# Attention over a 64 x 64 image: a ring buffer less for the column sums, half loads of v, and another order at the start

## The chip, the cores and the metric

The kernel runs on one core of one Trainium2 chip. The metric is the device time of one execution in microseconds (us). A core has five engines with an instruction queue each: TensorE (PE in the profile; its weight loads stand apart as PEld), VectorE (DVE), ScalarE (ACT), GpSimd (POOL) and SyncE (SP, which here only issues transfers). Transfers run on 16 DMA engines, which serve the queues of SP and ACT (hardware queues) and of POOL (a software queue).

## The reference

For each of 4 images, x has 4,096 pixels of 256 channels:

```python
q = jnp.einsum('bwhc,cd->bwhd', x, Wq) + bq      # 128 channels
k = jnp.einsum('bwhc,cd->bwhd', x, Wk) + bk      # 128 channels
v = jnp.einsum('bwhc,cd->bwhd', x, Wv) + bv      # 256 channels
pq, pk, pv = (t.reshape(B, -1, N) for t in (q, k, v))
energy = jnp.einsum('bcn,bcm->bnm', pq, pk)      # 4096 x 4096
attention = jax.nn.softmax(energy, axis=-1)
out = jnp.einsum('bcm,bnm->bcn', pv, attention).reshape(B, W, H, C)
return gamma * out + x
```

All is float32.

## The kernel before

**Three forms.** TensorE multiplies in a reduced format (fp32r). To keep accuracy each operand is held in three forms: an upper part h, a lower part l and a mixed part d. Each logical product becomes three products, one for each form, added up in PSUM. `split` (L152) makes the forms: ScalarE writes h, VectorE l and d (in the first image's later blocks GpSimd writes d).

**The main loop** (L700) has 512 steps, `n`: 4 images of 8 column groups (512 queries each) of 16 steps (256 keys each, as two halves `i` of 128). A step takes about 4.56 us. For the keys two steps ahead, `cross` (L350) and `energy` (L359) multiply keys and queries, and ScalarE takes the exponential into `x`; `upper` and `halves` make its forms h, l, d. For the keys of the step, `attend(n, j)` (L416) multiplies the forms by v's and adds into two banks, `a` (h and l) and `b` (d), for each half `j` of the columns. In `attend` the forms come in the order h, l, d, and in each form the halves of the keys come in the order 0, 1: six products.

**Turns.** At the last step of each column group (`turn`), `sum_forms` (L449) makes the upper and lower form of the sums of the exponentials, `zf`; the next step multiplies them by ones (`sums`, L459), and `finish` (L469) divides, adds x and stores. The code emits `next(zf)`, ScalarE's upper form, ahead of that step's projection work and of its exponentials, so all of these stand behind it in ScalarE's queue.

**The next image's projection** is spread over the loop: `step(p, engine)` (L557) does the p-th piece, 16 steps for two blocks of 256 pixels. At r = 7 and 8 of the 16 `qk_forms` (L295) begins the forms of q and k of the two blocks, at r = 11 and 13 `v_pair_forms` (L318) those of the two halves of v. From step 18 on r is one behind the step in its column group, so a turn falls on r = 14; in the first column group it falls on r = 13. All of these tiles, and `zf`, come from one ring of two buffers, tag `"pf"`. A finished tile is noted in `stores` and written to DRAM by SyncE in the next step (`store`, L325); a buffer is free again when its store has landed.

**Loads.** GpSimd issues the loads of the main loop: k of one step (`load_k`, three buffers) five steps ahead; q of a column group (`load_q`, L333, a ring of two, tag `"q"`) in the seventh step of the group before; v of the next image (`load_v`, L330) during the last column group of an image, one tile a step, as each tile of `vall` has had its last use. A tile of `vall` is [128, 2, 3, 256]: two key halves, three forms, 256 columns. The k loads wait for the products that read the buffer.

**The start** (L602 to L643) loads the weights and the first blocks, multiplies ones by ones on TensorE (`warm`), makes the weights' forms (`weights`, L167) and the first block's, and begins its products (`products`, L239). The biases of q and k are spread over the partitions by a product with ones into `bb`, v's by four products with one column. `x_forms` (L220) of the block i = 2 has VectorE write l, and GpSimd d. Then 16 blocks follow (L644), which project the first image.

Of the kernel before, what the change touches and what calls it, by code (L numbers as in the profile page):

```python
# [9 lines left out]
F32 = mybir.dt.float32  # L10
F32R = mybir.dt.float32r
I32 = mybir.dt.int32
AF = mybir.ActivationFunctionType
# [7 lines left out]
def kernel(  # L21
# [79 lines left out]
    with ExitStack() as fast:  # L101
# [22 lines left out]
        nc.scalar.dma_start(raw[:, 0, :, C2:], wk.rearrange("(k p) d -> p k d", p=P))  # L124
        nc.sync.dma_start(raw[:, 1], wv.rearrange("(k p) e -> p k e", p=P))
        nc.gpsimd.memset(zs, 1.0)
        rows = work.tile([P, 2, XB], F32, tag="pf", name="rows")[:1]
        rows = rows.rearrange("p s f -> p (s f)")
        make_identity(nc, ident)
        nc.vector.tensor_scalar(ones_r, zs.to_broadcast([P, P]), 1.0, None, ALU.mult)  # L130
        nc.scalar.dma_start(rows[:, :C2], bq.unsqueeze(0))
        nc.scalar.dma_start(rows[:, C2:C], bk.unsqueeze(0))
        nc.scalar.dma_start(rows[:, C:], bv.unsqueeze(0))
        nc.scalar.activation(zs, zs, AF.Exp)
        wp = ps_e.tile([P, P], F32, tag="e", name="wp")

# [62 lines left out]
        def load_x(b, i):  # L199
            if b == B or i >= NI:  # L200
                return
            if b == 0:
                t = xs4[:, i % 4]
                if i:
                    nc.sync.dma_start(t, xv[b, i])
                loads["x", b, i] = t
                return
            pair = work.tile([P, 2, 2, XB], F32, tag="xd", name=f"x_{b}_{i}", bufs=1)
            for u in range(2):
                nc.sync.dma_start(pair[:, u], xv[b, i + u])  # L210
                loads["x", b, i + u] = pair[:, u]

        def transposed(b, i):
            xs = loads.pop(("x", b, i))
            tp = units["xt", b, i] = bank(f"xt_{b}_{i}", [P, KC, 2, P], b, 0)
            for k in range(KC):
                for s in range(2):
                    nc.tensor.transpose(tp[:, k, s, :], xs[:, s, k * P : (k + 1) * P], ident)  # L218

        def x_forms(b, i):  # L220

            y = units.pop(("xt", b, i))
            if b == 0:
                if i % 3 < 2:
                    f = ppool.tile([P, 3, KC, 2, P], F32R, tag="ld", name=f"xf_{b}_{i}")
                else:
                    f = work.tile([P, 4, KC, 2, P], F32R, tag="xf", name=f"xf_{b}_{i}", bufs=1)
                f = [f[:, j] for j in range(3)]
            else:
                if i % 2 == 0:  # L230
                    shape = [P, 2, KC, 2, 2, P]
                    f = work.tile(shape, F32R, tag="xf", name=f"xf_{b}_{i}", bufs=1)
                    d = work.tile([P, *shape[2:]], F32R, tag="xd", name=f"xd_{b}_{i}", bufs=1)
                    now["xf"] = [f[:, 0], f[:, 1], d]
                f = [y_[:, :, i % 2] for y_ in now["xf"]]
            units["xf", b, i] = f
            yield from split(*f, y, b == 0 and i > 1)

        def products(b, i, w, fs):  # L239

            xf = units["xf", b, i]
            if fs[0] == 2:
                units[w, b, i] = bank(f"qv{w}_{b}_{i}", [P, 2, C], b, 1)
            to = units[w, b, i]
            for s in range(2):
                for f in fs:
                    for k in range(KC):
                        if w:
                            left, right = wf[:, 1, f, k, s * P : (s + 1) * P], xf[f][:, k]
                        else:  # L250
                            left, right = xf[f][:, k, s, :], wf[:, 0, f, k]
                        nc.tensor.matmul(  # L252
                            to[:, s, :],
                            left,
                            right.rearrange("p s a -> p (s a)") if w else right,
                            start=(f == 2 and s == k == 0),
                            stop=(f == 1 and k == KC - 1),
                            skip_group_check=True,
                        )
# [68 lines left out]
            stores.clear()  # L328

        def load_v(b, t):  # L330
            nc.gpsimd.dma_start(vall[:, t], vf[b, t])

        def load_q(b, g, j=None):  # L333
            if not j:
                loads["q", b, g] = work.tile([P, NJ, 3, P], F32R, tag="q", name=f"q_{b}_{g}")
            j = slice(NJ) if j is None else j
            nc.gpsimd.dma_start(loads["q", b, g][:, j], qd[b, g][:, j])

# [77 lines left out]
        def attend(n, j, order=(0, 1, 2)):  # L416

            t = n % NU
            if t == 0:
                for i, c in enumerate("ab"):  # L420
                    pool, tag = ps_o, f"{c}{j}"
                    if j and n >= (B - 1) * STEPS and n // NU % 2 == 0:
                        pool, tag = now["banks"][i]
                    now[c, j] = pool.tile([P, NB], F32, tag=tag, name=f"{c}{j}_{n // NU}")
            for f in order:
                to = now["ab"[f == 2], j]
                for i in range(2):
                    nc.tensor.matmul(  # L428
                        to,
                        vall[:, t, i, f, j * P : (j + 1) * P],  # L430
                        units[n][f][:, i, :],
                        start=(t == 0 and i == 0 and f != 1),
                        stop=(t == NU - 1 and i == 1 and f != 0),
                        skip_group_check=True,
                    )

# [12 lines left out]
        def sum_forms(n):  # L449

            s = now["total"] = now["sum"]
            f = work.tile([P, 2, NB], F32R, tag="pf", name=f"zf_{n // NU}")
            h, l = now["z"] = f[:, 0, :], f[:, 1, :]
            nc.scalar.activation(h, s[:, 0, :], AF.Identity, scale=UPPER)
            yield
            nc.vector.tensor_tensor(l, s[:, 0, :], h.bitcast(F32), ALU.subtract)
            yield
# [155 lines left out]
        now["turn"], now["banks"] = 0, [(ps_p, "p0"), (ps_p, "p1")]  # L613
        rings = cycle(now["banks"]), cycle([(ps_o, tag) for tag in ("a0", "b0", "a1", "b1")])
        image(0)
        f3 = work.tile([P, 2, 2, 3, P], F32R, tag="q", name="f3")
        for i in range(4):
            load_x(0, i)
        transposed(0, 0)
# [5 lines left out]
        next(x0)  # L625
        next(x0)
        next(w0)
        next(w1)
        products(0, 0, 0, (2,))
        bb = ps_e.tile([P, KC + C], F32, tag="e", name="bb")  # L630
        nc.tensor.matmul(bb[:, KC:], ones[:1], rows[:, :C], start=True, stop=True)
        nc.scalar.activation(bias, bb[:, KC:], AF.Identity, scale=REST)
        seed_qk(0, 0)
        transposed(0, 1)
        load_x(0, 4)
        x1 = x_forms(0, 1)
        next(x1)
# [6 lines left out]
        for i in range(NI):  # L644
            products(0, i, 0, (0, 1))
            qk = qk_forms(0, i)
            next(qk)
            if i == 0:
                for eh in range(KC):
                    nc.tensor.matmul(  # L650
                        bb[:, eh : eh + 1],
                        rows[:, C + eh * P : C + (eh + 1) * P],
                        ones[:1, :1],
                        start=True,
                        stop=True,
                    )
                nc.scalar.activation(bvs, bb[:, :KC], AF.Identity, scale=REST / E)
                products(0, 0, 1, (2,))
                seed_v(0)
                transposed(0, 2)  # L660
                load_x(0, 5)
                x2 = x_forms(0, 2)
                next(x2)
            if i + 1 < NI:
                products(0, i + 1, 0, (2,))
                seed_qk(0, i + 1)
            next(qk)
            next(qk)
            next(qk, None)
            if i == 0:  # L670
                next(x2)
            products(0, i, 1, (0, 1))
            vs = v_forms(i)
            next(vs)
            next(vs)
            next(vs, None)
            if i + 1 < NI:
                products(0, i + 1, 1, (2,))
                seed_v(i + 1)
            if i + 3 < NI:  # L680
                transposed(0, i + 3)
                for _ in x_forms(0, i + 3):
                    pass
            load_x(0, i + 6)
            store()
            if i in (7, 10):
                cross(i // 9)
            elif i in (8, 11):
                energy(i // 9)
            elif i in (9, 12):  # L690
                upper(i // 10)
            elif i == 14:
                halves(0)
            if 1 <= i <= NJ:
                load_q(0, 0, i - 1)
            if i in (2, 4, 6):
                load_k(i // 2 - 1)
            elif i in (8, 11):
                load_k(3 + i // 9)
# [277 lines left out]
```

## Time and profile before

| | us |
|---|---|
| median of three runs | 2379.47 |
| lowest and highest | 2377.36, 2379.63 |
| the profiled execution | 2377.93 |
| its span, first to last instruction | 2376.0 |

The page gives each engine's busy time and instructions, the span in 40 slices, the transfers by queue, the chain of work that ended last, and the costliest groups of instructions. In a row of the timeline the first two numbers are start and duration in us, and the brackets hold how long the engine had stood idle before it and what ended that. A wait row names who waited for whom, the total in us, the times and the longest. A row of the windows view gives the busy time of each engine in a stretch with the number of its instructions, the granted share of TensorE's clock, the busy share of the DMA engines and their rate. Matmuls are pipelined and their ends modelled, so the count of products in a stretch says more than the busy time.

| group | count | mean ns |
|---|---|---|
| a product of 128 x 512, `attend` | 6144 | 391 (they overlap) |
| exponential, 128 x 512, ACT | 960 | 596 |
| forms l and d of a step, 128 x 1024, DVE | 480 each | 1223, 1220 |
| load of k, POOL, 384 KB | 512 | 532 to issue |
| load of v, POOL, 768 KB | 48 | 536 to issue |

### The profile page before, as it was taken

The numbers are of one execution on the slowest core, as the hardware profiler recorded it, in microseconds if no ns is written. First come the engines' busy times: TensorE is split into PE (matmuls) and PEld (weight loads), VectorE is DVE, ScalarE is ACT, GpSimd is POOL, SyncE is SP. The second block draws the span as 40 slices with busy tenths as digits, with TensorE's granted clock in tenths as the row PEclk, the third lists the DMA queues.
The fourth block names the chain that finished last, engine by engine and source line by source line (L and its number), as shares of the span: only waits on it lengthen the run. The fifth ranks groups of instructions, "written<-read, shape, count | busy, mean of one in ns | idle before, by whom it ended". The sixth has DMA issues, their size and how long they took to land.

```text
span 2376.0 us, 31544 instructions
## 1 busy us (share of the span) xinstructions
PE 2353.1 (99%) x10822; PEld 1943.2 (82%) x10822; DVE 2127.3 (90%) x2098; ACT 1853.7 (78%) x3027; POOL 389.4 (16%) x665
## 2 busy tenths in 40 slices
PE   9999999999999999999999999999999999999998
PEld 8878888888878888888887888888888888888887
DVE  7988999989989899999888999999988988888888
ACT  6778777787777877778777787777887787887885
POOL 6211111111211111111121111111112111111110
PEclk9999999999999999999999999999999999999999
DMA  7556655556875565556696566654569644444453
GB/s 252 176 151 175 185 159 149 169 163 183 293 220 166 165 183 170 153 149 177 174 321 202 154 171 180 171 162 144 169 177 328 187 127 122 127 131 111 133 135 95
DMA packets 185674, 413.66 MB, mean 174 GB/s; under 512 B 26754, under 2 KB 77189, under 8 KB 185508
## 3 DMA queue, kind: packets, MB, share of 16 engines
q0 software_dynamic: 94144, 280.53, 43.5%
q1 hardware_dynamic: 90814, 130.77, 15.7%
q8 instruction: 89, 1.46, 0.3%
q14 instruction: 77, 0.63, 0.1%
q10 hardware_dynamic: 550, 0.26, 0.0%
HBM read 306.51 MB, written 104.98 MB: 173 GB/s over the span
## 4 chain that ended last, share of the span: by engine, by line
PE 89%; ACT 5%; DMA 2%; DVE 2%; issue 1%; SPq 0%; POOL 0%; ACTq 0%; DVEq 0%
PE a L428 36%; PE e L371 18%; PE b L428 18%; PE e L356 9%; PE qv L252 5%; PE v L269 2%; ACT x L374 2%; ACT o L442 1%; DVE ld L405 1%; PE xt L218 1%; DMA vf<-vf 1%; DMA qd<-f 1%; ACT e L357 1%; ACT h L380 1%; DVE ld L407 0%
## 5 line engine op out<-in xcount | busy, mean ns | idle before, releaser
L374 ACT ACTIVATE x<-e 128x512 f32<-128x512 f32 x960 | 522.6, 596 | 299.3 <-PE e L371 299.3
L405 DVE TENSOR_TENSOR ld<-x,h 128x1024 fp32r<-128x1024 f32 x480 | 586.9, 1223 | 96.1 <-ACT h L380 49.0
L391 DVE TENSOR_TENSOR s<-s,x 128x1024 f32<-128x1024 f32 x480 | 587.3, 1224 | 87.0 <-ACT x L374 84.5
L357 ACT ACTIVATE e<-e 128x512 f32<-128x512 f32 x1024 | 547.3, 573 | 137.4 <-PE e L356 137.2
L428 PE MATMUL a<-ld,v 128*128 128x512 f32 x2048 | 634.4, 391 | 1.2 <-DVE ld L405 0.3
L428 PE MATMUL a<-h,v 128*128 128x512 f32 x2048 | 635.0, 391 | 0.2
L428 PE MATMUL b<-ld,v 128*128 128x512 f32 x2048 | 632.1, 390 | 0.6 <-DVE ld L407 0.5
L343 POOL DMA_DIRECT2D k<-kf x512 | 272.3, 532 | 1930.2 <-PE e L371 1803.2
L407 DVE SCALAR_TENSOR_TENSOR ld<-h,x 128x1024 fp32r<-128x1024 f32 x480 | 585.8, 1220 | 0.0
L371 PE MATMUL e<-q,k 128*128 128x512 f32 x2048 | 554.2, 392 | 1.1
L380 ACT ACTIVATE h<-x 128x1024 fp32r<-128x1024 f32 x480 | 511.0, 1065 | 13.3
L371 PEld LDWEIGHTS e<-q,k 128*128 128x128 f32 x2048 | 380.3, 188 | 95.6 <-ACT e L357 19.9
L428 PEld LDWEIGHTS a<-ld,v 128*128 128x128 f32 x2048 | 383.0, 188 | 89.9 <-DVE ld L405 10.5
L428 PEld LDWEIGHTS b<-ld,v 128*128 128x128 f32 x2048 | 384.5, 188 | 82.7 <-issue 1.1
L428 PEld LDWEIGHTS a<-h,v 128*128 128x128 f32 x2048 | 379.6, 188 | 76.1 <-ACT o L442 1.3
L356 PE MATMUL e<-q,k 128*128 128x512 f32 x1024 | 317.8, 391 | 8.4 <-ACT x L374 7.1
L356 PEld LDWEIGHTS e<-q,k 128*128 128x128 f32 x1024 | 192.1, 188 | 52.0 <-ACT x L374 9.9
L305 DVE SCALAR_TENSOR_TENSOR f<-f,qv 128x512 fp32r<-128x512 f32 x128 | 85.9, 681 | 2.2 <-ACT f L302 2.0
L252 PE MATMUL qv<-wf,xf 128*128 128x256 f32 x576 | 79.2, 289 | 1.7 <-POOL xf L160 0.8
L252 PEld LDWEIGHTS qv<-wf,xf 128*128 128x128 f32 x576 | 75.4, 195 | 5.1 <-POOL xf L160 1.0
L164 DVE SCALAR_TENSOR_TENSOR vf<-vf,v 128x512 fp32r<-128x512 f32 x96 | 65.4, 682 | 5.9 <-ACT vf L154 5.8
L405 DVE TENSOR_TENSOR ld<-s,h 128x1024 fp32r<-128x1024 f32 x32 | 39.2, 1226 | 29.7 <-ACT h L380 28.2
(90 smaller groups left out, 1137.8 us busy)
## 6 DMA issues: line engine op xcount, KB each, us to landing
k<-kf POOLq DMA_DIRECT2D x512, 384.0 KB, 3.4
vf<-vf SPq DMA_DIRECT2D x96, 384.0 KB
v<-vf POOLq DMA_DIRECT2D x48, 768.0 KB, 6.9
kf<-f SPq DMA_DIRECT2D x128, 192.0 KB
qd<-f SPq DMA_DIRECT2D x128, 192.0 KB
q<-qd POOLq DMA_DIRECT2D x31, 768.0 KB, 4.8
o<-in_x_dram POOLq DMA_DIRECT2D x31, 512.0 KB, 7.2
out_dram<-o SPq DMA_DIRECT2D x31, 512.0 KB
```

Source lines behind the costliest of these rows:

```text
L252: nc.tensor.matmul(to[:, s, :], left, right.rearrange("p s a -> p (s a)") if w else right, start=(f == 2 and s == k == 0), stop=(f == 1 an ...
L305: nc.vector.scalar_tensor_tensor(f[:, :, :, j, :], h.bitcast(F32), s, y, ALU.mult, op)
L343: nc.gpsimd.dma_start(t, kf[b, u % NU])
L356: nc.tensor.matmul(e, *forms(n, i, 2), start=True, stop=False, skip_group_check=True)
L357: nc.scalar.mul(e, e, -REST)
L371: nc.tensor.matmul(e, *forms(n, i, f), start=False, stop=(f == 1), skip_group_check=True)
L374: nc.scalar.activation(x[:, i, :], e, AF.Exp, scale=(1.0 + E) ** 3 / E)
L380: nc.scalar.activation(h, units[n], AF.Identity, scale=UPPER)
L391: nc.vector.tensor_tensor(s, s, x, ALU.add)
L405: nc.vector.tensor_tensor(l, x, h.bitcast(F32), ALU.subtract)
L407: nc.vector.scalar_tensor_tensor(d, h.bitcast(F32), 1.0 + E, x, ALU.mult, ALU.subtract)
L428: nc.tensor.matmul(to, vall[:, t, i, f, j * P : (j + 1) * P], units[n][f][:, i, :], start=(t == 0 and i == 0 and f != 1), stop=(t == NU - ...
```

## The change

- In `attend`, l's two products come with the key halves in the order 1, 0; h's and d's stay at 0, 1.
- `q` has two fixed tiles, `qs`, in place of the ring of two. Column group G uses `qs[G % 2]`, and `zf` of the group is written into the first 1,024 columns of that tile, in place of a buffer of `"pf"`. The third tile of forms at the start, `f3`, is `qs[1]`.
- `load_v` issues two loads, one for each key half.
- At the start, v's bias is loaded directly to the partitions by two loads at the head of GpSimd's work and scaled by GpSimd, in place of four products and a ScalarE instruction; the product that spreads the biases of q and k, and ScalarE's copy of it, come ahead of the second weights and the first four products; one more warming product stands after the second block's transposes; and VectorE's second piece of the third block's forms comes ahead of the next block's products.

```diff
-        rows = work.tile([P, 2, XB], F32, tag="pf", name="rows")[:1]
-        rows = rows.rearrange("p s f -> p (s f)")
+        for eh in range(KC):
+            nc.gpsimd.dma_start(bvs[:, eh : eh + 1], bv[eh * P : (eh + 1) * P].unsqueeze(1))
+        rows = work.tile([P, XB], F32, tag="pf", name="rows")[:1]
...
-        nc.scalar.dma_start(rows[:, C2:C], bk.unsqueeze(0))
-        nc.scalar.dma_start(rows[:, C:], bv.unsqueeze(0))
+        nc.scalar.dma_start(rows[:, C2:], bk.unsqueeze(0))
...
         def load_v(b, t):
-            nc.gpsimd.dma_start(vall[:, t], vf[b, t])
+            for i in range(2):
+                nc.gpsimd.dma_start(vall[:, t, i], vf[b, t][:, i])
 
         def load_q(b, g, j=None):
-            if not j:
-                loads["q", b, g] = work.tile([P, NJ, 3, P], F32R, tag="q", name=f"q_{b}_{g}")
+            loads["q", b, g] = qs[g % 2]
...
-                for i in range(2):
+                for i in (1, 0) if f == 1 else (0, 1):
                     nc.tensor.matmul(
...
-                        stop=(t == NU - 1 and i == 1 and f != 0),
+                        stop=(t == NU - 1 and f != 0 and i == f // 2),
...
         def sum_forms(n):
 
             s = now["total"] = now["sum"]
-            f = work.tile([P, 2, NB], F32R, tag="pf", name=f"zf_{n // NU}")
-            h, l = now["z"] = f[:, 0, :], f[:, 1, :]
+            f = qs[n // NU % 2].rearrange("p j f a -> p (j f a)")
+            h, l = now["z"] = f[:, :NB], f[:, NB : 2 * NB]
...
-        f3 = work.tile([P, 2, 2, 3, P], F32R, tag="q", name="f3")
+        qs = [work.tile([P, NJ, 3, P], F32R, tag=f"q{g}", name=f"q{g}", bufs=1) for g in range(2)]
+        f3 = qs[1].rearrange("p (s w) f a -> p s w f a", s=2)
...
         next(w0)
+        bb = ps_e.tile([P, C], F32, tag="e", name="bb")
+        nc.tensor.matmul(bb, ones[:1], rows, start=True, stop=True)
+        nc.scalar.activation(bias, bb, AF.Identity, scale=REST)
         next(w1)
+        nc.gpsimd.tensor_scalar(bvs, bvs, REST / E, None, ALU.mult)
         products(0, 0, 0, (2,))
-        bb = ps_e.tile([P, KC + C], F32, tag="e", name="bb")
-        nc.tensor.matmul(bb[:, KC:], ones[:1], rows[:, :C], start=True, stop=True)
-        nc.scalar.activation(bias, bb[:, KC:], AF.Identity, scale=REST)
         seed_qk(0, 0)
         transposed(0, 1)
+        warm(1)
...
             if i == 0:
-                for eh in range(KC):
-                    nc.tensor.matmul(
-                        bb[:, eh : eh + 1],
-                        rows[:, C + eh * P : C + (eh + 1) * P],
-                        ones[:1, :1],
-                        start=True,
-                        stop=True,
-                    )
-                nc.scalar.activation(bvs, bb[:, :KC], AF.Identity, scale=REST / E)
                 products(0, 0, 1, (2,))
                 seed_v(0)
                 transposed(0, 2)
                 load_x(0, 5)
                 x2 = x_forms(0, 2)
+                next(x2)
                 next(x2)
...
-            if i == 0:
-                next(x2)
             products(0, i, 1, (0, 1))
```

## The prediction

> **What bounds the kernel now.** I read the page first: shares by engine, then the chain by engine.
>
> ```profile
> PE 2353.1 (99%) x10822; PEld 1943.2 (82%) x10822; DVE 2127.3 (90%) x2098; ACT 1853.7 (78%) x3027; POOL 389.4 (16%) x665
> ...
> PE 89%; ACT 5%; DMA 2%; DVE 2%; issue 1%; SPq 0%; POOL 0%; ACTq 0%; DVEq 0%
> ```
>
> TensorE is busy nearly all the time, so an edit beside it is worth nothing unless TensorE waits for it. But the chain holds 2% of transfers, some 47 us in which a transfer and not TensorE set the order. The waits of ScalarE (ACT), in columns total, times, longest, say which, and the timeline and the chain at those places say what it costs.
>
> ```profile
> ACT zf L454 <- DMA vf<-vf: 8.3, 3, 4.8
> ACT vf L154 <- DMA qd<-f: 8.2, 5, 2.8
> ...
> 143.99 0.60 ACT L154 ACTIVATE vf<-v 128x512 fp32r<-128x512 f32 x1 [2.06 <-DMA vf<-vf]
> ...
> 1248.96 0.63 ACT L454 ACTIVATE zf<-s 128x512 fp32r<-128x512 f32 x1 [4.75 <-DMA vf<-vf]
> 1250.13 1.28 PE L356 MATMUL e<-q,k 128*128 128x512 f32 x2 [3.75 <-ACT x L374]
> ...
> 1236.60 12.29 DMA vf<-vf
> ...
> 1818.66 14.05 DMA qd<-f
> ...
> 47.12 0.93 PE e L371 x4
> ...
> 1254.13 1.71 PE e L371 x4
> ```
>
> At 1249 ScalarE stood 4.75 us in front of the column sums' upper form (zf), which wanted a "pf" buffer that a store of v (vf) still read; the exponentials queued behind it, and TensorE idled 3.75 us. Afterwards four products took 1.71 us where they take 0.93: the clock had been halved. At 144 the form of v, pushed on by zf in the ring of two, waited in the same way. The stretches around these places, each above a quiet one at a whole number of column groups' distance (73 us a group), give the loss; columns are length, PE busy with its products, clock, share and rate of the DMA engines.
>
> ```profile
> 142.00:153.90 11.90, 10.57 (x42) 1.00 0.40 130
> 215.00:226.90 11.90, 11.85 (x51) 1.00 0.53 165
> 640.00:648.00 8.00, 7.51 (x32) 1.00 1.09 392
> 713.00:721.00 8.00, 8.00 (x37) 1.00 0.87 259
> 655.00:670.00 15.00, 13.01 (x47) 0.89 0.92 327
> 728.00:743.00 15.00, 14.95 (x65) 1.00 0.55 180
> 1244.00:1261.00 17.00, 13.25 (x46) 0.80 0.80 287
> 1317.00:1334.00 17.00, 16.95 (x75) 1.00 0.60 180
> 1756.00:1763.00 7.00, 7.00 (x33) 1.00 0.57 167
> 1829.00:1836.00 7.00, 5.78 (x25) 1.00 1.09 410
> ```
>
> **zf in q's dead buffer.** Products missing, times the quiet stretch's time of one: at 142, 9 x 0.23 = 2.1 us; at 655, 18 x 0.23 = 4.1; at 1244, 29 x 0.226 = 6.6. The clock's part is inside these counts. In the new place zf waits for the last product that read this group's q, issued two steps earlier (keys run two steps ahead), and the next q comes into it seven steps later, behind the sums' product: neither is late. The ring then turns over two tiles of q and k and two of v in sixteen steps, and each reuses a tile begun four or more steps before; zf's was begun three before, and its store issued one before. All three losses go: **-12.8**. Less than nothing is excluded, since no wait is added that ends later; at most 12.8, as every other turn already runs without loss. The 144 case needs no congestion, only the order in the ring, so it is the surest.
>
> What is late next is the ring's remaining wait: the forms of v behind stores of q and k, 8.2 us in five waits. TensorE lost (37 - 32) x 0.216 = 1.1 there at 640 and (33 - 25) x 0.212 = 1.7 at 1829. These stay in q's part of the edit, and the halves below bear on them.
>
> **v loaded by halves.** One load of 768 KB becomes two of 384 KB, 48 more on POOL's queue. What the queues do at the batch edges (1810 to 1833) and in a quiet stretch (300 to 323), the queue rows being packets, MB, share:
>
> ```profile
> q0 software_dynamic: 1577, 6.01, 76.5%
> q1 hardware_dynamic: 1573, 2.52, 32.6%
> ...
> v<-vf POOLq DMA_DIRECT2D x5, 768.0 KB, 8.5
> k<-kf POOLq DMA_DIRECT2D x5, 384.0 KB, 6.3
> ...
> k<-kf POOLq DMA_DIRECT2D x6, 384.0 KB, 3.3
> ...
> L331 POOL DMA_DIRECT2D v<-vf x48: 528/536/563, 602.0 to 1850.9; - x48
> L428 PE MATMUL a<-ld,v x2048: 387/389/628, 71.8 to 2367.6; 128*128 128x512 f32 x187
> L428 PEldq EVENT_SEMAPHORE  x37: 51/51/51, 69.9 to 2302.2; - x37
> ```
>
> Both queues moved the same number of packets (1577 and 1573) with 6.01 MB against 2.52: they take turns by packet, and the stores' packets are small. A row of v is one packet of 6 KB; halved, it is two of 3 KB, the size of k's, and the stores get a turn after each. So stores land sooner at the edges and loads later. The five loads' 640 rows make 1577 packets 2217, and their mean falls from 3.8 KB to 2.7; with a store's 1.6 KB a pair of turns falls from 5.4 to 4.3, and the 14 us from issue to use at 1832 to some 11, about the 2.8 us (longest) that was waited. The losses of 1.1 and 1.7 would go at best and stay at worst: between 0 and -2.8, I take **-1.2**. [...] The equal counts agree with the turns; if a turn were many rows long, halving rows would change nothing and this term would be 0 instead of -1.2.
>
> The price: 48 x 0.536 = 26 us more on POOL, hidden because POOL is busy 16% and no load of v is due within ten steps; uncovered it would push k's next load by half a microsecond. k lands 6.3 us after its issue at an edge, 3.3 in quiet; it is issued in one step and used three starts later, some 10 us on (a step is 73/16 = 4.56), so it has 3 to 4 us to spare. TensorE gets up to 48 more waits of 0.051 us: 0 to +2.4; the 37 of now open no gap in the quiet stretches, since weights are loaded ahead, so **0**.
>
> **l's products in the other order.** All are the same instruction, 389 ns in the middle, on operands that VectorE finishes in one piece, and d's products still come last, so nobody's release moves. Their shortest is 387; 2 ns on 1,024 pairs are 2 us, so I bound it by -2 and +2 and take **0**, where the middle is.
>
> **The start.** Timeline rows, then one of the chain:
>
> ```profile
> 1.48 0.71 POOL L142 DMA_DIRECT2D gam<-in_L_conv_gamma_dram  x1 [0.16 <-issue]
> ...
> 7.15 1.22 PE L252 MATMUL qv<-wf,xf 128*128 128x256 f32 x4 [0.56 <-DVE xf L164]
> ...
> 8.30 1.22 PE L631 MATMUL bb<-rows,ones 1*128 1x256 f32 x2
> ...
> 9.97 0.70 DVE L280 SCALAR_TENSOR_TENSOR qv<-qv,bias 128x512 f32<-128x512 f32 x1 [1.68 <-ACT bias L632]
> ...
> 10.73 2.08 PE L252 MATMUL qv<-wf,xf 128*128 128x256 f32 x8 [0.16 <-DVE qv L280]
> ...
> 12.73 1.01 PE L650 MATMUL bb<-ones,rows 1*128 1x1 f32 x4
> ...
> 14.70 1.05 PE L218 MATMUL xt<-ident,xs 128*128 128x128 f32 x4
> ...
> 19.21 1.28 POOL L160 TENSOR_TENSOR xf<-xf 128x512 fp32r<-128x512 f32 x1 [10.54 <-DVE xf L157]
> 20.54 0.74 PE L252 MATMUL qv<-wf,xf 128*128 128x256 f32 x4 [0.82 <-POOL xf L160]
> ...
> 23.16 2.87 PE qv L252 x24
> ```
>
> The bias product (1.2) moves ahead of the first four: 0.56 fills idle time, so these start at 7.8 and end near 8.8. The bias is ready by then, VectorE's seed runs 8.8 to 9.5, beside it TensorE transposes (0.9) and does the one warming product (0.4), and the eight products start near 10.0 instead of 10.73: -0.7. The four small products for v's bias go: -0.9. VectorE does the third block's l before the next seed, and POOL's d moves from 19.21 to about 16: the wait of 0.8 before 20.54 goes, and about 0.2 of weight loading with it: -1.0. Against that, TensorE runs at half rate here (eight products 2.08, later 24 in 2.87); 1.6 us of work moved before the full clock costs 0.8 more. Sum -1.8 if the full clock comes when it did; about -3.0 if TensorE, now without the hole before 10.73, has it from 14 on, so that the 0.8 isn't lost and the block's second half runs faster too. The two bias loads on POOL (0.71 each by gamma's row) put off the identity to about 2.9, before its use at 4.6; if they delayed x's load too, some 0.5 would be lost. Range -0.5 to -3.5, taken: **-2.0**. [...]
>
> **Sum.** The profiled execution took 2377.9 (span 2376.0 and 1.9 around it): 2377.9 - 12.8 - 1.2 - 2.0 = 2361.9. The median of the runs shown is 1.5 above that execution, the lowest 0.6 below; taking half of it gives **2362.7**.
>
> **The rivals.** (1) The ring's other wait takes over: at each edge v's form waits for the stores of q and k with TensorE idle 1.7 us and the clock halved once more (the 1.71 us row, some 1.7 us lost). For it: those waits exist, and engines at 1.09 are full. Against it: halves help the stores. Two edges give back 7 us: 2370.
> (2) Slower: k comes late. POOL's queue now yields a turn to the stores at every 3 KB, and k stands behind v in it. It decides once k lands over 10 us after issue, where 6.3 is seen; 16 steps at three edges, each late by 1 us, cost 48 us: 2410, and 0.33 us each already eats the gain. Against it: stores bring only 2.52 MB to POOL's 6.01, so what they gain early they don't take later.
> (3) Nothing is gained: the edges are bound by transfers (0.92 and 1.09 of the engines' time), and the idle time comes back behind the next load; the start's 2.0 alone is left: 2376. Against it: 728 and 1317 run full with 0.55 to 0.60, and just outside the stalls TensorE never waits for a load.
>
> **How the numbers follow.** Forecast 0.73 (its own range 2357 to 2368: start and stores at their ends), rival 1 0.14, rival 2 0.07, rival 3 0.06. From 2357, a little below the sum of the best ends (2377.9 - 12.8 - 2.8 - 3.5 = 2358.8), to 2373, past rival 1, holds about 8 in 10. A measurement of this kernel can tell 0.2%, 4.8 us; faster is then 0.73 + 0.14 = 0.87, within it 0.06, slower 0.07.
>
> **What would show it.** Right: no zf wait on a store, the stretches at 144, 658 and 1246 full of products, the clock undipped there; v's loads 96, stores at the edges sooner, k's landing under 8 us; eight products near 10.0 and no wait on POOL near 19. Wrong: ScalarE still waiting for stores at the turns, TensorE waiting for k, or the products' spacing changed where l's order turns.

## The result, and the profile after

The changed kernel takes 2356.93 us in the median of five runs (2356.55 to 2359.12) against 2379.47: ratio 0.9911, 95% interval 0.9897 to 0.9926, or 21 us less (18 to 24) by all runs; the two medians lie 22.5 apart. The forecast was 2362.7, 17 us less; the measured time stands at the very low end of the range, 2357, and 0.1 us past it.

The page of the changed kernel, first the shares and then the chain by engine:

```profile
PE 2340.9 (99%) x10820; PEld 1937.3 (82%) x10820; DVE 2126.2 (90%) x2098; ACT 1852.4 (79%) x3026; POOL 416.8 (18%) x716
...
PE 95%; ACT 2%; DVE 1%; issue 1%; POOL 1%; DMA 0%; DVEq 0%; POOLq 0%; ACTq 0%
```

The chain's 2% of transfers are gone, and TensorE's part rose from 89% to 95%. The waits of ScalarE hold no wait of the column sums' form for a store any more; of its waits for transfers these two are the longest (total us, times, longest):

```profile
ACT f L302 <- DMA qd<-f: 2.4, 2, 1.5
...
ACT vf L154 <- DMA qd<-f: 1.4, 3, 0.7
```

The first of them stands in the projection of the first image (at 32.6 and 56.3 us), so that in the main loop the 1.4 us of the second are all that is left.

The stretches of the main loop in which the kernel before lost products, found again by their place in the order of work (they come earlier now), in the windows view with TensorE alone:

```profile
135.00:146.90 11.90, 11.86 (x51) 1.00 0.54 181
633.00:641.00 8.00, 8.00 (x37) 1.00 1.13 385
646.90:661.90 15.00, 14.96 (x69) 1.00 1.14 405
1231.50:1248.50 17.00, 16.96 (x77) 1.00 1.09 380
1809.70:1816.70 7.00, 7.00 (x33) 1.00 1.13 406
```

All five are full, with the whole clock. In the last four the DMA engines are at least as full as before (1.09 to 1.14, before 0.80 to 1.09), so full engines alone cost no time here: it matters who waits for them.

The start is the other part. The sixth transposes mark its end, since from there on both kernels take 3.3 us a block. Timeline rows, the kernel before and the changed one:

```profile
25.86 0.60 PE L218 MATMUL xt<-ident,xs 128*128 128x128 f32 x4
```

```profile
8.32 1.22 PE L252 MATMUL qv<-wf,xf 128*128 128x256 f32 x8 [0.29 <-DVE qv L280]
...
19.51 0.60 PE L218 MATMUL xt<-ident,xs 128*128 128x128 f32 x4
...
35.53 0.74 PE L252 MATMUL qv<-wf,xf 128*128 128x256 f32 x4 [1.22 <-POOL xf L160]
```

The start is 6.4 us shorter in these two executions, three times the forecast. Of that, 0.6 is there before any edit of TensorE's work can act: the first transposes began at 4.02 us in place of 4.65, and in the other executions at 4.2 to 4.6. The eight products began at 8.32, where I had put 10.0, and took 1.22 and not 2.08: TensorE had its full rate from 6.1 us on, not from 17.1. Some of it is given back at 35.53, where TensorE now waits for GpSimd.

To add up the parts I took, for every product from 64 us on, its distance to the next one beyond the quiet distance (0.227 us for 512 columns) and summed. That leaves out the start and counts each stall and each halved clock once.

| kernel | lost in the main loop, us | time, median, us |
|---|---|---|
| before | 42.3 | 2379.47 |
| sums' forms in q's tile alone (e1) | 29.8 | 2367.76 |
| half loads alone (e2) | 42.2 | 2376.79 |
| the start alone (e4) | 44.1 | 2375.07 |
| all but the half loads (e5) | 30.4 | 2361.94 |
| all but the start (e9) | 26.4 | 2360.73 |
| changed | 25.7 | 2356.93 |

Each loss is that of one execution. In three more with the main loop of before (e3, e7, e11) it is 42.5 to 45.9, in four more with that of the changed kernel (e6, e8, e10, e12) 26.0 to 26.5. The experiments' medians come from three sets, and the kernel before, run beside each, had 2377.4 to 2378.8 there.

### The profile page after: what moved, and what is told of

The parts are those of the page before. It is cut to its first block, busy times and chain, and to the rows that moved or that the text cites. A ratio compares the mean times of both kernels' runs of the same rounds, so it can differ in the third digit from the quotient of the medians.

```text
span 2354.9 us, 31737 instructions
## 1 busy us (share of the span) xinstructions
PE 2340.9 (99%) x10820; PEld 1937.3 (82%) x10820; DVE 2126.2 (90%) x2098; ACT 1852.4 (79%) x3026; POOL 416.8 (18%) x716
## 4 chain that ended last, share of the span: by engine, by line
PE 95%; ACT 2%; DVE 1%; issue 1%; POOL 1%; DMA 0%; DVEq 0%; POOLq 0%; ACTq 0%
PE a L428 39%; PE e L371 20%; PE b L428 19%; PE e L356 10%; PE qv L252 4%; PE v L269 3%; PE xt L218 1%; ACT o L442 1%; ACT x L374 1%; PE z L466 1%; ACT e L357 0%; DMA xs<-in_x_dram 0%; DVE ld L405 0%; ACT h L380 0%; POOL v L160 0%
## 5 line engine op out<-in xcount | busy, mean ns | idle before, releaser
L380 ACT ACTIVATE h<-x 128x1024 fp32r<-128x1024 f32 x480 | 511.0, 1065 | 13.2
L371 PEld LDWEIGHTS e<-q,k 128*128 128x128 f32 x2048 | 379.4, 188 | 94.8 <-ACT e L357 19.9
L428 PEld LDWEIGHTS a<-ld,v 128*128 128x128 f32 x2048 | 382.5, 188 | 90.2 <-DVE ld L405 11.1
L305 DVE SCALAR_TENSOR_TENSOR f<-f,qv 128x512 fp32r<-128x512 f32 x118 | 79.2, 679 | 2.5 <-ACT f L302 2.2
```

Of the source, the lines that this page charges most:

```text
L305: nc.vector.scalar_tensor_tensor(f[:, :, :, j, :], h.bitcast(F32), s, y, ALU.mult, op)
L371: nc.tensor.matmul(e, *forms(n, i, f), start=False, stop=(f == 1), skip_group_check=True)
L380: nc.scalar.activation(h, units[n], AF.Identity, scale=UPPER)
L428: nc.tensor.matmul(to, vall[:, t, i, f, j * P : (j + 1) * P], units[n][f][:, i, :], start=(t == 0 and i == 0 and f != 1), stop=(t == NU - ...
```

## The experiments

**e1: the sums' forms in q's tile, alone.**

```diff
-            f = work.tile([P, 2, NB], F32R, tag="pf", name=f"zf_{n // NU}")
-            h, l = now["z"] = f[:, 0, :], f[:, 1, :]
+            f = qs[n // NU % 2].rearrange("p j f a -> p (j f a)")
+            h, l = now["z"] = f[:, :NB], f[:, NB : 2 * NB]
```

(with `qs`, `f3` and `load_q` as in the change)

> The kernel before with one part of the change: the sums' forms in q's tile, everything else as before. Theory: the three losses at the turns (9, 18 and 29 products missing around 144, 655 and 1244) go, and the other waits for stores of q and k stay: 12.8 us less, about 2366. Rival (the halves of v do it, by landing the stores sooner): only the loss at 144, which needs no full DMA engines, is sure to go; 2 to 4 us less, and the stall near 1246 comes back at another tile of the ring.

Measured: 2367.76 (2360.99 to 2369.34), ratio 0.9950 (0.9934 to 0.9966), 12 us less. In the windows view of e1 the stretch at the turn after the first image and that after the second are full, those at the other waits are not:

```profile
637.00:645.00 8.00, 7.30 (x31) 1.00 1.09 394
652.00:667.00 15.00, 14.95 (x69) 1.00 1.06 357
1233.00:1250.00 17.00, 16.92 (x76) 1.00 1.09 397
1807.00:1814.00 7.00, 6.09 (x26) 1.00 1.09 394
```

The row of zf is gone from ScalarE's waits, and that of v's forms behind the stores of q and k is what it was (8.2 before):

```profile
ACT vf L154 <- DMA qd<-f: 8.7, 5, 3.0
```

The theory holds, in size (12.8 forecast, 12.5 by the table, more against the other executions of before) and in what stays.

**e2: half loads of v, alone.**

```diff
-            nc.gpsimd.dma_start(vall[:, t], vf[b, t])
+            for i in range(2):
+                nc.gpsimd.dma_start(vall[:, t, i], vf[b, t][:, i])
```

> The kernel before with v loaded by halves alone. Theory: the losses at 640 and 1829 (1.1 and 1.7 us) shrink to under 1 together, the zf waits shrink by the share that the stores land sooner (14 to some 11 us from issue to use), but do not vanish: 2 to 6 us less. Rival (halves remove the zf waits themselves): the turns at 658 and 1246 run full, 12 to 14 us less. Rival (halves only delay k or cost TensorE waits): no change or up to 3 us more.

Measured: 2376.79, ratio 0.9988 (0.9979 to 0.9997). The waits of ScalarE and the windows around the first three turns' stalls, in e2:

```profile
ACT zf L455 <- DMA vf<-vf: 12.6, 4, 6.0
...
ACT vf L154 <- DMA vf<-vf: 2.3, 1, 2.3
...
ACT vf L154 <- DMA qd<-f: 1.5, 3, 0.7
```

```profile
137.00:148.90 11.90, 10.29 (x42) 1.00 0.46 151
651.00:666.00 15.00, 10.88 (x36) 0.77 0.87 307
1241.00:1258.00 17.00, 12.56 (x44) 0.80 0.90 311
```

The waits for stores of q and k (8.2 us before, line 154) shrank to 1.5, and none cost TensorE a third of a microsecond. But the sums' form waited longer for v's stores, 12.6 us against 8.3, not shorter as the theory had it. By the table the main loop lost 42.2 us as before; that compares two executions, though. Summed by place, e2 lost nothing at the third edge, where the five executions with the main loop of before lost 1.7 to 4.7 us, and 6.6 and 6.8 at the first two, where those lost 5.2 to 6.9. So the halves alone gain something at the third edge and leave the turns as they were. That fits the 3 us of the ratio; how much of them is theirs, and how much the start's (this execution had the full clock early, below), is not shown.

**e3: l's products in the other order, alone.**

```diff
-                for i in range(2):
+                for i in (1, 0) if f == 1 else (0, 1):
```

> The kernel before with l's two products in the other order alone. Theory: nothing, within 1 us of the kernel before, and products of l at 389 ns as before. Rival (the order costs or saves time in each of the 1,024 attends): 5 us or more either way, with the spacing of l's products off by 5 ns or more.

Measured: 2379.32, ratio 1.0001 (0.9991 to 1.0010). In e3's view of the line that holds these products (shortest, middle and longest in ns), l's products (and d's of the other bank) are what they were:

```profile
L428 PE MATMUL a<-ld,v x2048: 387/389/628, 71.4 to 2368.6; 128*128 128x512 f32 x187
L428 PE MATMUL b<-ld,v x2048: 388/389/628, 72.5 to 2365.6; 128*128 128x512 f32 x187
```

No difference is shown, within 2.4 us either way.

**e4: the edits of the start, alone** (the change without the hunks of e1, e2 and e3).

> The kernel before with the edits of the start alone. The changed kernel's start is 6.4 us shorter by the fourth transposes (19.5 for the group that was at 25.9), where 2.0 was forecast. Theory: the edits keep TensorE busy without a hole, so the full rate is there from about 6 to 10 us instead of 17: 5 to 6.5 us less, near 2373.5. Rival (the changed kernel's profiled execution had the clock early by chance, as x's first load also came 0.6 us sooner): 1.8 to 3 us less, and the full rate of the profiled execution comes after 10 us.

Measured: 2375.07 (2371.51 to 2380.71), ratio 0.9988 (0.9979 to 0.9997): 3 us less, 1 to 5. The full rate came at 4.4 us and the sixth transposes at 19.9, so the profiled execution has the early clock of the theory, and the median is that of the rival. (What the expectation calls the fourth transposes are the sixth.) A likely reason is in the clock's table below: the kernel before does not always have the clock late.

**e5: all but the half loads.**

```diff
-            for i in range(2):
-                nc.gpsimd.dma_start(vall[:, t, i], vf[b, t][:, i])
+            nc.gpsimd.dma_start(vall[:, t], vf[b, t])
```

> The changed kernel with v loaded whole again. Theory: the two stalls behind stores of q and k come back (0.86 and 1.07 us of TensorE near 640 and 1810, as with the sums' forms alone), with their following gaps 2 to 4 us more than the changed kernel's 2357, so 2359 to 2361. Rival (halves only worked because of the turns' stalls): no difference, 2357.

Measured: 2361.94 (2360.34 to 2363.84), ratio 0.9936 (0.9922 to 0.9949), 5 us over the changed kernel. The waits of ScalarE and of TensorE in e5:

```profile
ACT vf L154 <- DMA qd<-f: 10.3, 6, 3.5
```

```profile
PE e L355 <- ACT x L373: 2.0, 2, 1.4
...
PE e L355 <- ACT s L373: 0.5, 1, 0.5
```

With the turns free, the forms of v wait 10.3 us for the stores of q and k, and TensorE stood still in three places, 0.7 us at 636, 1.6 at 1222 and 0.6 at 1817. With halves (the rows of the changed kernel above) 1.4 us of that wait are left and no stall. From the records of the transfers I took the time from the issue of a block's four stores of q and k to their last packet, for the six blocks at the edges:

| | first edge | second | third |
|---|---|---|---|
| before | 13.4, 14.1 | 9.7, 13.3 | 11.8, 14.8 |
| e5, whole loads | 13.2, 13.8 | 13.6, 15.3 | 11.4, 14.2 |
| changed, half loads | 10.7, 12.4 | 11.1, 12.2 | 10.8, 12.6 |

This is the forecast mechanism (14 to 11 us); its worth was not 1.2 us but 4.7 by the table of losses (e5 to the changed kernel), or 3.4 (e1 to e9). What it costs stands in the transfers view of the changed kernel at the third edge (1790 to 1813):

```profile
q0 software_dynamic: 2189, 5.78, 77.6%
q1 hardware_dynamic: 1585, 2.55, 34.6%
...
v<-vf POOLq DMA_DIRECT2D x11, 384.0 KB, 8.8
k<-kf POOLq DMA_DIRECT2D x5, 384.0 KB, 7.6
```

k lands 7.6 us after its issue instead of 6.3, within its 10.

**e6: all but l's order** (e3's hunk undone in the changed kernel).

> The changed kernel with l's products in the old order. Theory: 2357, no difference. Rival (the order matters together with the half loads, since the first products after a load then wait for one half at a time): 1 to 4 us more, with gaps behind h's products in the steps that follow a load of v.

Measured: 2358.48 (2356.73 to 2359.70), ratio 0.9918 (0.9905 to 0.9932), which overlaps the changed kernel's interval; the losses in the main loop are 26.0 us, against 25.7. No difference is shown. This execution had its full clock at 10.4 us.

**The clock at the start.** The table has, for each profiled execution, when TensorE first got its full rate, when it lost it again, when it had it for the rest of the start, and the start of the sixth transposes, in us. The first is the first record of the granted clock; ahead of it the windows view has none and prints 1.00, but the products tell the rate: in the kernel before, eight took 2.08 us ahead of it (at 10.73) and 24 took 2.87 after it (at 23.16).

| start | kernel | first | lost | for good | sixth transposes |
|---|---|---|---|---|---|
| as before | before | 17.1 | | 17.1 | 25.9 |
| | e11, before again | 5.7 | 9.1 | 16.0 | 24.7 |
| | e1 | 6.1 | 9.5 | 16.3 | 24.4 |
| | e2 | 4.2 | | 4.2 | 21.8 |
| | e3 | 17.4 | | 17.4 | 25.6 |
| | e9 | 4.6 | 8.0 | 18.2 | 24.4 |
| holes filled | e7 | 5.7 | | 5.7 | 21.9 |
| new | changed | 6.1 | | 6.1 | 19.5 |
| | e12, changed again | 6.0 | | 6.0 | 19.8 |
| | e4 | 4.4 | | 4.4 | 19.9 |
| | e5 | 5.6 | | 5.6 | 19.8 |
| | e6 | 10.4 | | 10.4 | 21.2 |
| | e10 | 10.4 | | 10.4 | 21.0 |
| new, with holes | e8 | 10.2 | | 10.2 | 20.6 |

**e7 and e8: do holes make the clock late?** e7 fills the start of the kernel before with warming products, e8 takes them from the changed kernel.

```diff
-        warm(6)
+        warm(7)
...
-        warm(2)
+        warm(4)
...
         transposed(0, 1)
+        warm(2)
```

> The kernel before with the three holes of TensorE's start filled by five more warming products (one at the beginning, two before the first products, two after the second transposes), nothing else changed. Theory (the late clock is the holes' doing): the full rate comes by 7 to 10.5 us, the sixth transposes start near 22 instead of 25.9, 2 to 3.5 us less, 2375.5 to 2377. Rival (chance): as likely late as before, no change on the median.

```diff
-        warm(2)
...
-        warm(1)
```

> The changed kernel without the three warming products between the first transposes and the first eight products, so that TensorE stands idle there some 0.9 us. Theory: the full rate comes after 10 us in most executions, and the start is 1.5 to 4 us longer: 2358.5 to 2361. Rival (the work moved and removed is all that counts, the clock is chance): 2357, or 0.4 us less, as a warming product less stands before the eight products.

Measured: e7 2378.38, ratio 1.0000 (0.9991 to 1.0009); e8 2358.22 (2357.39 to 2362.31), ratio 0.9922 (0.9909 to 0.9936), overlapping the changed kernel's. e7's profiled execution does what the theory says, its median doesn't; e8's is between the two. Holes as such are not shown to decide it.

**e9: all but the start** (e1's, e2's and e3's hunks together).

> The sums' forms in q's tile, half loads and l's order, with the start as before. Theory: turns and edges account for 12 + 4.7 us and the start for 3 or more, so about 2361 (16.5 us less than before), with no gap of TensorE over 0.5 us between 74 and 2340. Rival (the parts add up only with the new start): 2363 or more, with stalls left at the edges.

Measured: 2360.73 (2358.56 to 2361.58), ratio 0.9929 (0.9913 to 0.9944), 17 us less, and no stall over 0.4 us from 74 us on. The parts of the main loop add up, and the start is worth the 3.8 us between this and the changed kernel (3.4 to e12, run beside it). The windows view of e9's start, in stretches of 3.4 us, and then that of the changed kernel's:

```profile
4.60:8.00 3.40, 2.30 (x15) 0.99 0.91 301
8.00:11.40 3.40, 3.15 (x14) 0.50 0.32 95
11.40:14.80 3.40, 3.40 (x17) 0.50 0.01 3
```

```profile
2.70:6.10 3.40, 3.38 (x16) 1.00 0.81 261
6.10:9.50 3.40, 3.11 (x21) 1.00 0.72 237
9.50:12.90 3.40, 3.24 (x28) 1.00 0.43 133
```

In e9 the full rate came at 4.6, TensorE was then busy 2.3 of 3.4 us, and the granted clock was 0.50 from 8.0 to 18.2. In the changed kernel TensorE was busy 3.1 of the 3.4 us after its full rate had come, and the clock stayed at 1.00. So the old start often lost what it had got early (three of the four executions with an early rate), the new one in none of six.

**e10: the first q's loads one block later**, against the new wait at 35.53.

```diff
-            if 1 <= i <= NJ:
-                load_q(0, 0, i - 1)
+            if 2 <= i <= NJ + 1:
+                load_q(0, 0, i - 2)
```

> The changed kernel with the four loads of the first q each issued one block later. In the changed kernel GpSimd stood 1.6 us in front of such a load at 31.85, behind the store it reads, and TensorE then idled 1.4 us at 34.0 for a form that GpSimd makes. Theory: that gap goes, 1.0 to 1.4 us less than the changed kernel, 2355.5 to 2357. Rival (the store itself is late and ScalarE's wait for it takes over): the gap stays at another engine, 2357 to 2358.

Measured: 2362.27 (2361.83 to 2362.80), ratio 0.9937 (0.9922 to 0.9951): 5 us worse than the changed kernel, outside both expectations. The gap at 34 is gone, but the first energies now wait for q and come 3.5 us later, in e10's timeline and then in the changed kernel's:

```profile
37.60 0.60 PE L218 MATMUL xt<-ident,xs 128*128 128x128 f32 x4
41.56 0.80 PE L356 MATMUL e<-q,k 128*128 128x512 f32 x1 [3.37 <-DMA q<-qd]
```

```profile
38.02 0.70 PE L356 MATMUL e<-q,k 128*128 128x512 f32 x2
```

The loads had been early for that reason: the products of the first keys need all of q. After this wait the clock was halved from 41.2 to 44.6 us (the execution's mean is 0.998, the changed kernel's 0.999); and a part of the 3.5 us is the full clock's coming at 10.4 and not at 6.1 in this execution (the sixth transposes are at 21.0 and not at 19.5).

**e11 and e12: both kernels once more**, for the clock.

> The kernel before once more, for the time at which TensorE gets its full rate. Chance theory: anywhere from 4 to 17.5 us, with the sixth transposes between 21.8 and 25.9. Rival (the holes always make it late): at 16 to 17.5 again.

> The changed kernel once more, for the same. Chance theory: anywhere from 4 to 10.5 us, the sixth transposes between 19.5 and 21.2. Rival (no holes, so always early): by 6.5 us, the sixth transposes near 19.6. Both: no zf wait, no gap of TensorE over 0.5 us between 74 and 2330.

Measured: 2380.33 and 2357.28, one run each; their clocks stand in the table. e11 has the numbers of both (for good at 16.0, transposes at 24.7) and the course of neither: the rate came early and was lost again. e12 has those of its rival, but e6 and e10, without the holes too, had the rate at 10.4, so that "always early" does not hold.

## Why the prediction was right, and where a size was off

- **zf in q's tile, -12.8.** Right in place, cause and size: -12 by e1, and the stretches at 144, 658 and 1246 are full in it.
- **What is late next.** Right: the forms of v behind stores of q and k. This wait was 8.7 us in e1 and 10.3 in e5. Both lack the stall at 1246, so that what made e5's longer stays open.
- **Half loads, -1.2 (0 to -2.8): mis-sized.** The mechanism was right (stores 14 to some 11 us, k later by 1.3 us, POOL's added issues hidden). Its worth is 3.4 to 4.7 us. The sum took less than half of the 1.1 and 1.7 us that it had found at two edges, where with halves both go whole; and once the turns are free all three edges cost TensorE time, 3.2 us together in e1 and 4.3 in e5. The second edge, which the sum had at nothing, cost 0.2 in e1 and 2.1 in e5. Alone the halves did less (e2), as the wait for v's own stores did not shrink. The equal counts on which the reading of the turns rested were partly luck, since that view holds stretches in which one queue had no work; the same view of the changed kernel has 2189 and 1585. In a stretch in which both had work the counts of rows were 1,137 and 1,151 (last section), which agrees with the reading; how many rows a turn holds they don't tell.
- **l's order, 0.** Right (e3, e6).
- **The start, -2.0 (-0.5 to -3.5): mis-sized.** By the executions with the full rate kept from early on, 21.8 and 21.9 against 19.5 to 19.9, the moved and removed work is worth 2.1, near the 1.8 of the step by step sum. What it lacked is the clock: the sum took one execution's 17.1 us for the rule. Its other value, -3.0, rests on a full clock at 14 once the hole before 10.73 is gone, an estimate that no run shows: with the new start it came at 4.4 to 10.4. The old start has it at 16 to 18 us in five of six, mostly after losing it, the new one earlier. Against this comes the new wait of 1.2 us for GpSimd at 35.53, which the sum did not have. The net is -3 (e4) to -3.8 (e9 against the changed kernel). Why the clock comes early or late in an execution stays open. That the warming product has a part in it is not shown.
- **Rival 1**, the ring's other wait taking over, is what e1 and e5 show at the edges without the half loads, at 0.6 to 1.6 us a place, though without the halved clock that it feared (1.00 in e1's stretches; e5's mean granted clock is 0.999, as the changed kernel's). **Rival 2** had the right sign for k, 7.6 for 6.3 us, and did not decide. **Rival 3** fell: full DMA engines (1.09 to 1.14) and a full TensorE (8.00 of 8.00 us at 633) stand side by side in the same stretches.

The sum with the measured sizes: 12.5 for the sums' forms, 4.7 for the halves on top of it, 3 to 3.8 for the start, 20 to 21 of the 21 us measured. What the forecast lacks of the measurement (5.8 us) is in the main these two sizes: 3.5 for the halves, 1 to 1.8 for the start.

## What to carry to other kernels

Look in the waits for an engine that stands in front of a buffer which a store still reads, and count what is queued behind it: 10 us of such waits (8.3 and 2.1) cost 12.5 of time here, since TensorE's granted clock was 0.50 as well, for 3.4 us at one turn (from 662.2) and 6.8 at the next (from 1249.3). A ring shared by short-lived and stored tiles can be relieved by any buffer that is dead at that moment. When one wait goes, price the next one anew (here 3.4 to 4.7 us in place of 1.2), and before moving a load away from a wait look up its first reader, which cost e10 5 us.

## What the runs showed of the hardware that was not expected

- The full rate of TensorE was lost 3.4 us after it was granted in e1, e9 and e11 (at 9.5, 8.0 and 9.1 us): TensorE was busy 2.2 to 2.4 of the 3.4 us, idle for 1.0 to 1.2 in all, and the granted clock was then 0.50 for 6.8 to 10.2 us. It is not that share alone: in e2 it was busy 1.99 of the 3.4 us after the grant and kept the rate. What tells them apart stays open.
- Two queues that both had work moved nearly the same number of rows, not of bytes. In the changed kernel's records from 1794 to 1808 us, in which both had work all the time, the software queue moved 1,137 rows of 3 KB and the hardware queue 1,151 of 1.5 or 2 KB. With v's rows at 3 KB in place of 6 KB on one queue, at the same number of bytes, the stores of q and k on the other took 10.7 to 12.6 us at the edges and not 11.4 to 15.3. v's stores, in rows of 3 KB themselves, did not get sooner (at the second edge 12.1 us from issue to the last packet before, 12.8 in e2); why is open.
